# A two-layer metaformer on one core: another order of the pipeline's steps, other phases of the scan, one cast moved from GpSimd to VectorE

## The chip, the cores and the metric

One core of a Trainium2 chip runs the whole kernel. The metric is the device time of one execution in microseconds (us). The engines are called as in the profile: PE is TensorE's matmuls and PEld its weight loads, DVE is VectorE, ACT is ScalarE, POOL is GpSimd, SP is SyncE, which here only issues DMAs.

## The reference

The input x has shape (32, 56, 56, 96): 32 images of 56 by 56 positions with 96 channels. Two layers follow, each a mixing part and a feed-forward part with residual additions:

```python
# layer 0
x = x + L0_conv(ln_c(x))     # shifted 7x7 window attention, 3 heads of 32 channels
t = t + L0_ffn(ln_t(t))      # t: x as tokens
# layer 1
x = x + L1_conv(ln_c(x))     # layer norm, expansion to 192 channels, gate, scan along the width
t = t + L1_ffn(ln_t(t))
```

The attention rolls the image by three positions, makes q, k and v, adds a position bias to the scores, takes a softmax over the 49 positions of a window and projects the result. The feed-forward part rounds its operands to an 8-bit float, does 96 to 384 channels, relu, and 384 back to 96, with sums rounded to 16 bits:

```python
y = q_acc(einsum('bsk,nk->bsn', q_mul(x), q_mul(W)))
return q_acc(y + q_mul(b))
```

The scan of layer 1 is, for each image row and each of 192 channels, `state = state * A + u * B; y = sum(state * C)` over 56 columns. The result is multiplied by a sigmoid gate and projected back to 96 channels.

## The kernel before

**Tiles.** Each image is cut into four blocks of 14 rows, so there are 128 blocks of 784 positions. A block lies in one SBUF tile xb (128 partitions x 7 x 96, fp32), of which there are 14. It is loaded once, passes all steps of both layers in place, and is stored.

**Steps and shifts.** The work on one block is cut into about a hundred named steps. Each has a shift, written behind its name in the table PIPELINED: in tick t the step works on block t minus its shift. A tick goes through the table once, from front to back. The program is fully unrolled, and `in_order` fixes the order on each engine to that of the table. So a step early in the table with a shift of 2 runs beside steps of blocks that are 4, 6, 10 or 13 behind. The largest shift is 13, so the table is gone through 142 times; 13 ticks at each end fill and drain the pipeline.

**The names.** The letters a, f, e and g stand for the four layer norms: attention, first feed-forward, scan, second feed-forward. For each of them, s is the statistics (DVE, L535), m the subtraction of the mean (L541), n the multiplication with the root (L555), t the transposition into PSUM (PE, tr_a, tr_f, tr_e, tr_g: L217 or L566), and e or, for the scan, xe the copy out of PSUM (ACT; xe is L882 and writes xs). R0 to R7 compute the reciprocal roots of all four norms of a tick on DVE in eight small instructions (L509 to L517). The other steps are:

- Attention: q, k and v (PE, L616 and L635), eq, ek and ev (ACT copies, L628 and L646), sc (scores, L658, which takes two bank pairs), st0 to st2 (DVE, L687), ex0 to ex2 (ACT exponentials, L700), av (PE, L738), rc and an (DVE, L756 and L764), tro (PE, tr_o, L217), eo (ACT, L780), pr (PE, L793), ad (DVE adds pr to xb, L586).
- Feed-forward, with f or g behind the first letter: hf0 to hf2 (PE, ph_f, L815), xf (ACT cast to 16 bits, L827), rf (DVE bias and relu on the 16-bit tile h_f, L833), cf (cast to the 8-bit tile hq, L839), yf (PE, py_f, L849), zf (ACT, L861), bf and kf (additions, L867 and L871).
- Scan: pu0 to pu3 (PE, L896), th and uc (ACT out of pu into gt and u, L911 and L917), SC0 to SC5 (PE, the scan as matmuls with a Toeplitz matrix, L939), GA0 to GA5 (DVE, gate times scan, L959), gt0 and gt1 (PE transposition), eg1 and eg0 (ACT, L982), so (PE, L992), "as" (DVE adds so to xb, L586).
- LD loads a block and ST stores one, each with six or nine DMAs on SP's queue.

**Which engine.** ON_GPSIMD names the steps of the kinds m, n, c, b and k that POOL does. All others of these kinds are DVE's. Before, POOL does mf, nf, me, ne, ng, cf0, cf1, cf2 and kf.

**PSUM.** There are four pairs of PSUM banks (NPS = 4). When a PE step is put into the program, `banks` gives it the pair at the front of a free list. EMPTIES says after which step a pair is free again; then it goes to the end of that list. So the table also decides which emptying step a PE step has to wait for.

**The scan's phases.** A scan step SCn works on a window of four successive blocks at once, every fourth tick. PHASE gives, for each of the six groups of channels, at which block number modulo 4 the window begins. Phase 0 means that the window is one image. With any other phase it covers the end of one image and the beginning of the next, and the DVE step GA behind it needs four instructions instead of two. The tick of a scan step modulo 4 follows from its shift and its phase together.

**A second path.** The program contains another, unpipelined order (IN_TURN) behind a branch for weights of unusual size. It does not run on these inputs.

Of the kernel before, what the change touches and what calls it, by code (L numbers as in the profile page):

```python
# [52 lines left out]
ROOT_BITS = 1595932665.0  # L53
ROOT_STEPS = ((0.703952253, 1.681913974), (0.5, 1.50000032))

ON_GPSIMD = "mf nf me ne ng cf0 cf1 cf2 kf"


PIPELINED = (
    "xf0:4 xg0:13 bf:5 xg1:13 k:2 SC1:10 ne:6 ek:2 v:2 pr:3 GA1:10 ma:1 GA0:10 ad:3 q:2 te:6 hf2:4 sf:3 ev:2 "  # L60
    "eq:2 rf0:4 kf:5 mf:3 xe:6 sc:2 se:5 pu2:6 st0:2 xf2:4 st1:2 ex0:2 pu1:6 st2:2 ex1:2 R0:0 R1:0 rg1:13 "
    "ex2:2 th2:6 uc2:6 th1:6 rg0:13 uc1:6 gt1:10 gt0:10 R2:0 cg2:13 R3:0 cg0:13 av:2 eg1:10 hf1:4 rf2:4 "
    "tg:12 eg0:10 R4:0 pu0:6 cf0:4 cg1:13 R5:0 eg:12 mg:11 pu3:6 R6:0 R7:0 na:1 xf1:4 so:10 rc:2 an:2 nf:3 "
    "ta:1 rf1:4 cf2:4 uc0:6 th0:6 as:10 LD:0 sa:0 uc3:6 th3:6 tro:2 SC3:9 ea:1 SC2:9 SC4:9 ng:11 eo:2 SC5:9 "
    "tf:3 cf1:4 hg2:12 GA3:9 ef:3 xg2:12 sg:10 GA2:9 yg:13 GA5:9 GA4:9 yf:4 hf0:3 rg2:12 hg0:12 zg:13 bg:13 "
    "hg1:12 zf:4 me:5 kg:13 ST:13 SC0:9 "
)

IN_TURN = (
# [18 lines left out]
def kernel(  # L88
# [184 lines left out]
    ne = EH // 2  # L273
# [208 lines left out]
    def engine(name):  # L482
        return nc.gpsimd if name in ON_GPSIMD.split() else nc.vector

# [432 lines left out]
        nc.scalar.copy(dst, held["pu", i, j][:, 0:n, :, EH:].rearrange("p g r e -> p e g r"))  # L917


    PHASE = (3, 2, 1, 2, 3, 0)  # L920

    def window(n):
        return [i for i in range(n, n + NBLK) if 0 <= i < nblocks]
# [95 lines left out]
    def pipeline(text, track, one_bias):  # L1019
# [16 lines left out]
        for t in range(nblocks + 1 + max(lag for _, lag in table)):  # L1036
# [3 lines left out]
            for name, lag in table:  # L1040
                i = t - lag
                if name[0:2] in ("SC", "GA"):
                    due = (i - PHASE[int(name[2])]) % NBLK == 0 and window(i)
                elif name[0] == "R":
# [74 lines left out]
```

## Time and profile before

| | us |
|---|---|
| median of 3 runs | 3170.72 |
| lowest and highest run | 3163.45, 3171.2 |
| the profiled execution, its own time | 3165.43 |
| span of the profiled execution, first to last instruction | 3163.7 |
| PE busy in that span | 3042.9 |
| PEld, DVE, ACT, POOL busy | 2511.5, 2605.6, 2304.8, 1504.6 |

The granted TensorE clock was 0.989 of full speed in the mean.

A timeline row gives the start and the length of a group of like instructions in us, then engine, line, operation, out<-in with shapes, and the count; in brackets is the idle time of the engine before it and what ended it. A group's row gives its busy time in total and the mean length of one instruction in ns, then the idle time before it. A row of a stretch of time gives the stretch, its length, and the busy time of each engine.

### The profile page before, as it was taken

What the parts mean: (1) busy time and instruction counts of PE and PEld (TensorE: products, weight loads), DVE (VectorE), ACT (ScalarE), POOL (GpSimd) and SP (SyncE); (2) the same over time, 40 slices, a digit from 0 to 9 for tenths busy, and PEclk for the clock granted to TensorE, in tenths of its full rate; (3) what the DMA queues carried; (4) which work ended last, traced back from release to release, by engine and by line L of the source; (5) the groups of instructions that cost most, each with busy time, mean ns of one, the idle gap of its engine ahead of it and who ended that gap; (6) DMA issues with size and microseconds to landing.
All of it is one profiled execution on the core that took longest, in us unless ns stands there. A gap on an engine that the chain in (4) does not pass through costs nothing.

```text
span 3163.7 us, 180034 instructions
## 1 busy us (share of the span) xinstructions
PE 3042.9 (96%) x80228; PEld 2511.5 (79%) x80228; DVE 2605.6 (82%) x7149; ACT 2304.8 (73%) x4610; POOL 1504.6 (48%) x1219
## 2 busy tenths in 40 slices
PE   4999999999999999999999999999999999999996
PEld 3778888888888888888888888888888888888875
DVE  6778888888888888888888888888888888888876
ACT  2667777777777777777777777777777777777774
POOL 4555444445444445444444444544544544544540
PEclk8899999999999999999999999999999999999998
DMA  6000111111111111111111111111111111111001
GB/s 140 23 4 19 29 32 27 29 32 27 29 32 27 28 33 27 28 33 26 27 34 27 26 34 27 26 34 27 26 33 28 27 34 27 26 32 29 23 22 34
DMA packets 232640, 97.09 MB, mean 31 GB/s; under 512 B 225292, under 2 KB 231854, under 8 KB 231854
## 3 DMA queue, kind: packets, MB, share of 16 engines
q1 hardware_dynamic: 228410, 84.40, 11.5%
q8 instruction: 633, 10.37, 1.4%
q10 hardware_dynamic: 3444, 1.06, 0.2%
q14 instruction: 153, 1.25, 0.1%
HBM read 42.05 MB, written 43.35 MB: 27 GB/s over the span
## 4 chain that ended last, share of the span: by engine, by line
PE 90%; ACT 5%; DVE 2%; issue 2%; POOL 1%; DVEq 0%; ACTq 0%; DMA 0%; SPq 0%; POOLq 0%
PE pu L896 20%; PE so L992 10%; PE qk L616 9%; PE scan L939 7%; PE av L738 6%; PE pv L635 6%; PE s L658 5%; PE pr L793 5%; PE ph_g L815 4%; PE py_f L849 4%; PE py_g L849 4%; ACT qk L628 3%; PE gt L217 3%; PE ph_f L815 3%; PE tr_f L566 2%
## 5 line engine op out<-in xcount | busy, mean ns | idle before, releaser
L896 PE MATMUL pu<-weg,xs 128*64 128x192 f32 x7168 | 640.9, 330 | 4.1 <-ACT xs L882 3.5
L535 DVE BATCH_NORM_STATS2 stats<-xb 128x6 f32<-128x192 f32 x2048 | 578.1, 348 | 1.8 <-POOL xb L871 1.7
L555 POOL TENSOR_TENSOR xn_f<-xc_f,roots 128x672 fp8e5<-128x672 f32 x128 | 243.4, 1901 | 663.6 <-DVE roots L517 663.6
L896 PEld LDWEIGHTS pu<-weg,xs 128*64 128x64 f32 x7168 | 492.4, 137 | 81.4 <-ACT xs L882 6.0
L871 POOL TENSOR_TENSOR xb<-xb,y_f 128x672 f32<-128x672 f32 x128 | 239.3, 1870 | 464.6 <-DVE y_f L867 461.2
L541 POOL TENSOR_TENSOR xc_f<-xb,stats 128x672 f32<-128x672 f32 x128 | 181.6, 1419 | 426.9 <-DVE stats L535 270.2
L628 ACT COPY qk<-qk 128x392 f32<-128x392 f32 (+1 forms) x256 | 173.8, 679 | 231.9 <-PE qk L616 231.7
L992 PE MATMUL so<-wso,gT 128*64 128x96 f32 x7168 | 322.8, 248 | 4.8 <-ACT gT L982 4.8
L827 ACT CAST h_g<-ph_g 128x784 f16<-128x784 f32 x384 | 307.6, 856 | 27.3 <-PE ph_g L815 16.9
L827 ACT CAST h_f<-ph_f 128x784 f16<-128x784 f32 x384 | 318.4, 829 | 10.4 <-PE ph_f L815 10.4
L992 PEld LDWEIGHTS so<-wso,gT 128*64 128x64 f32 x7168 | 315.9, 138 | 10.2 <-ACT gT L982 5.4
L839 POOL CAST hq<-h_f 128x784 fp8e5<-128x784 f16 x384 | 320.3, 834 | 6.1 <-DVE h_f L833 6.1
L616 PE MATMUL qk<-xw,wqkv 128*32 128x196 f32 (+1 forms) x3072 | 304.8, 392 | 2.3 <-ACT h_f L827 2.3
L606 ACT COPY xw<-tr_a 96x392 f32<-96x392 f32 x256 | 117.4, 514 | 249.1 <-PE tr_a L217 212.6
L586 DVE TENSOR_TENSOR xb<-so,xb 128x384 f32<-128x384 f32 (+1 forms) x256 | 118.1, 503 | 188.8 <-PE so L992 188.8
L586 DVE TENSOR_TENSOR xb<-pr,xb 128x384 f32<-128x384 f32 (+1 forms) x256 | 118.1, 503 | 183.4 <-PE pr L793 183.4
L959 DVE SCALAR_TENSOR_TENSOR gt<-gt,scan 128x448 f32<-128x448 f32 (+2 forms) x694 | 236.5, 400 | 38.3 <-PE scan L939 38.1
L849 PEld LDWEIGHTS <-hq 128*128 128x128 fp8e5 x5376 | 246.7, 99 | 26.4 <-DVE hq L839 8.6
L939 PEld LDWEIGHTS scan<-u,toep 64*64 64x64 f32 x12288 | 200.1, 135 | 64.6 <-ACT xw L606 29.2
L939 PE MATMUL scan<-u,toep 64*64 64x56 f32 (+1 forms) x12288 | 221.6, 220 | 30.8 <-ACT xw L606 21.3
L917 ACT COPY u<-pu 128x384 f32<-128x384 f32 (+1 forms) x512 | 242.1, 473 | 4.5 <-PE pu L896 4.5
L911 ACT ACTIVATE gt<-pu 128x384 f32<-128x384 f32 (+1 forms) x512 | 237.8, 464 | 5.5 <-PE pu L896 5.5
(161 smaller groups left out, 6706.0 us busy)
## 6 DMA issues: line engine op xcount, KB each, us to landing
xb<-in_x_dram SPq DMA_DIRECT2D x224, 126.0 KB
out_dram<-xb SPq DMA_DIRECT2D x224, 126.0 KB
taps_d<-u SPq DMA_DIRECT2D x1, 4704.0 KB
xb<-in_x_dram SPq DMA_DIRECT2D x224, 13.1 KB
xb<-in_x_dram SPq DMA_DIRECT2D x224, 7.9 KB
out_dram<-xb SPq DMA_DIRECT2D x224, 13.1 KB
out_dram<-xb SPq DMA_DIRECT2D x224, 7.9 KB
xb<-in_x_dram SPq DMA_DIRECT2D x32, 72.0 KB
```

The source lines that it names most:

```text
L535: nc.vector.bn_stats(st[:, g : g + 2, :].rearrange("p g s -> p (g s)"), pair.rearrange("p g c -> p c g"))
L555: engine("n" + n).tensor_tensor(xn, xc, rs[:, :, None].to_broadcast([128, G, C]), ALU.mult, **saturate)
L616: nc.tensor.matmul(pq[j * rows : (j + 1) * rows, m, 0:size], wqkv[:, m * C + h0 * HD : m * C + h1 * HD], xws[i % 2][:, j * size : (j + 1) ...
L628: nc.scalar.copy(dst, held.pop(("qk", i, n)))
L827: nc.scalar.copy(h16.rearrange("p (h t) -> p h t", h=2), held.pop(("ph", n, i, hc))[:, :, 0:HALF])
L839: engine(f"c{n}{hc}").tensor_copy(hq[:, :, 0:HW], h16.rearrange("p (r w) -> p r w", w=HW), saturate=False)
L849: nc.tensor.matmul(po[:, g - g0, :], hq[hc][:, 2 * g : 2 * g + 2, :].rearrange("p r w -> p (r w)"), w2q[:, hc, :], start=(hc == 0), stop=( ...
L871: engine("k" + n).tensor_tensor(xtiles[i], xtiles[i], held.pop(("y16", n, i)), ALU.add)
L896: nc.tensor.matmul(pu[h * RS : (h + 1) * RS, g, r * E : (r + 1) * E], xs[:, 2 * j + g, r, :], weg[:, h, :], start=True, stop=True,)
L917: nc.scalar.copy(dst, held["pu", i, j][:, 0:n, :, EH:].rearrange("p g r e -> p e g r"))
L939: nc.tensor.matmul(py[o0 : o0 + RS, b, e, rows], toep[h * RS : (h + 1) * RS, ch * HW : ch * HW + RS], u[h * RS : (h + 1) * RS, ch, rows], ...
L992: nc.tensor.matmul(po[r * ROW : (r + 1) * ROW, g, :], gT[:, h, 2 * g + r, :], wso[:, h, :], start=(h == 0), stop=(h == 1),)
```

## The change

Three things differ; no instruction's form is new.

The table PIPELINED is another one, with the same step names. In it, all six scan groups have a shift of 9 (SC1, GA0 and GA1 had 10), v goes from 2 to 1, pr from 3 to 2, xf0 from 4 to 3, xg0 from 13 to 12, ne from 6 to 5, bf and kf from 5 to 4; most steps stand elsewhere in the order. PHASE has other values. ON_GPSIMD no longer names cf2, so that cast is DVE's.

```diff
-ON_GPSIMD = "mf nf me ne ng cf0 cf1 cf2 kf"
+ON_GPSIMD = "mf nf me ne ng cf0 cf1 kf"

 PIPELINED = (
-    "xf0:4 xg0:13 bf:5 xg1:13 k:2 SC1:10 ne:6 ek:2 v:2 pr:3 GA1:10 ma:1 GA0:10 ad:3 q:2 te:6 hf2:4 sf:3 ev:2 "
-    "eq:2 rf0:4 kf:5 mf:3 xe:6 sc:2 se:5 pu2:6 st0:2 xf2:4 st1:2 ex0:2 pu1:6 st2:2 ex1:2 R0:0 R1:0 rg1:13 "
-    "ex2:2 th2:6 uc2:6 th1:6 rg0:13 uc1:6 gt1:10 gt0:10 R2:0 cg2:13 R3:0 cg0:13 av:2 eg1:10 hf1:4 rf2:4 "
-    "tg:12 eg0:10 R4:0 pu0:6 cf0:4 cg1:13 R5:0 eg:12 mg:11 pu3:6 R6:0 R7:0 na:1 xf1:4 so:10 rc:2 an:2 nf:3 "
-    "ta:1 rf1:4 cf2:4 uc0:6 th0:6 as:10 LD:0 sa:0 uc3:6 th3:6 tro:2 SC3:9 ea:1 SC2:9 SC4:9 ng:11 eo:2 SC5:9 "
-    "tf:3 cf1:4 hg2:12 GA3:9 ef:3 xg2:12 sg:10 GA2:9 yg:13 GA5:9 GA4:9 yf:4 hf0:3 rg2:12 hg0:12 zg:13 bg:13 "
-    "hg1:12 zf:4 me:5 kg:13 ST:13 SC0:9 "
+    "ev:2 ma:1 q:2 ad:3 k:2 sf:3 xg1:13 te:6 hf2:4 rf0:4 se:5 eq:2 ek:2 sc:2 xe:6 R0:0 st2:2 xf2:4 ex2:2 "
+    "st0:2 pu2:6 st1:2 ex0:2 th2:6 pu0:6 uc2:6 rg0:13 R1:0 gt1:10 rg1:13 th0:6 mf:3 R2:0 ex1:2 me:5 cg2:13 "
+    "R3:0 cg1:13 R4:0 rf2:4 cg0:13 eg1:10 gt0:10 R5:0 eg0:10 uc0:6 pu1:6 th1:6 uc1:6 R6:0 av:2 LD:0 hf1:4 "
+    "tg:12 R7:0 so:10 eg:12 xf1:4 na:1 rc:2 an:2 mg:11 pu3:6 as:10 rf1:4 uc3:6 cf0:4 th3:6 cf2:4 hg2:12 ta:1 "
+    "sg:10 tro:2 SC3:9 xg2:12 SC4:9 ea:1 eo:2 GA3:9 SC5:9 SC0:9 GA0:9 GA4:9 nf:3 tf:3 GA5:9 yg:13 cf1:4 "
+    "hg0:12 yf:4 ne:5 ef:3 zg:13 rg2:12 xg0:12 zf:4 hg1:12 hf0:3 ng:11 sa:0 bg:13 SC2:9 kg:13 xf0:3 bf:4 "
+    "SC1:9 ST:13 v:1 kf:4 GA2:9 pr:2 GA1:9 "
 )
 
-    PHASE = (3, 2, 1, 2, 3, 0)
+    PHASE = (0, 0, 1, 2, 1, 3)
```

## The prediction

> **What bounds the kernel now.** First part 1 of the page, then two steady ticks out of the stretches' busy times, from one tr_e step to the next (columns after the length: PE, PEld, DVE, ACT, POOL busy with counts, granted clock, DMA).
>
> ```profile
> PE 3042.9 (96%) x80228; PEld 2511.5 (79%) x80228; DVE 2605.6 (82%) x7149; ACT 2304.8 (73%) x4610; POOL 1504.6 (48%) x1219
> 1514.34:1537.50 23.16, 22.86 (x595) 18.89 (x594) 19.39 (x54) 17.80 (x36) 11.69 (x9) 1.00 0.13 31
> 1537.50:1561.78 24.28, 23.97 (x659) 19.92 (x658) 20.67 (x58) 17.98 (x36) 11.14 (x9) 1.00 0.14 34
> ```
>
> PE is all but full at full clock; the second tick holds one scan more (1.09 us). Four such ticks (one period of the scans) take 23.16 + 24.28 + 24.24 + 23.18 = 94.86 us, 128 blocks 32 x 94.86 = 3036 us; the other 128 us of the 3163.7 us span are the filling and the draining.
>
> A busy PE hides short waits, because a matmul's modelled end runs on. So in the timeline I measure each step from its first matmul to that of the next step.
>
> ```profile
> 1514.34 0.55 PE L217 MATMUL tr_e<-ident,xc_e 56*96 56x56 f32 x14
> 1514.51 0.82 ACT L628 COPY qk<-qk 128x784 f32<-128x784 f32 x1 [1.72 <-PE qk L616]
> 1514.83 0.51 PE L815 MATMUL ph_f<-xq,w1q 128*128 128x392 fp8e5 x2
> 1515.22 1.24 ACT L882 ACTIVATE xs<-tr_e,bet,gam 96x392 f32<-96x392 f32 x2
> 1515.38 1.24 PE L658 MATMUL s<-qk 32*64 32x49 f32 x96
> ...
> 1521.66 0.51 PE L815 MATMUL ph_f<-xq,w1q 128*128 128x392 fp8e5 x2
> 1522.01 0.50 PE L566 MATMUL tr_g<-ident,xn_g 128*96 128x112 fp8e5 x7
> ...
> 1526.97 0.92 DVE L586 TENSOR_TENSOR xb<-so,xb 128x384 f32<-128x384 f32 x2 [1.33 <-PE so L992]
> 1527.24 0.54 PE L217 MATMUL tr_o<-ident,an 49*96 49x49 f32 x16
> 1528.04 1.15 PE L939 MATMUL scan<-u,toep 64*64 64x56 f32 x64 [0.26 <-DVE xb L586]
> ...
> 1531.96 0.83 PE L815 MATMUL ph_g<-xq,w1q 128*128 128x392 fp8e5 x4
> 1532.75 0.87 PE L616 MATMUL qk<-xw,wqkv 128*32 128x196 f32 x16
> ```
>
> Three waits return in every tick. Step hf2 takes 0.55 us before sc (1514.83 to 1515.38), hf1 only 0.35 (1521.66 to 1522.01): 0.21 us lost, because q stands two short steps ahead of sc and eq (0.82) is not done. tro takes 0.80 us where its shortest of 128 is 0.47: 0.33 lost, because the scan takes the banks that "as" empties (1526.97 + 0.92). hg0 and hg1 take 0.79 us where two such steps take 0.67: 0.12 lost at hg1, which waits for zg. Together 0.66 us a tick. All other steps have the same length, within about 0.01 us, in nearly all ticks: PE sets the pace and these waits are all that a new order can win in the steady part.
>
> **A rule of the Trainium skill beside this.** "Perfetto Trace Analysis", Identifying the Most-Contended Engine, says that matmul busy overstates how full TensorE is, and takes the weight loads' busy share instead: 18.89 of 23.16 us. By that, up to 4.27 us a tick (547 us) would be open. The rows decide otherwise: steps do not get shorter when neighbours change, so the sum uses 0.66 us.
>
> **The change, part by part.** The words speak of three exchanges; the list ON_GPSIMD loses one name, cf2. All else is order.
>
> Scans. Six windows per four ticks before and after, but in ticks of 3, 1, 1, 1 before and 2, 2, 1, 1 after; two of them now cover one image instead of one. An unsplit window's two instructions of 606 ns cost DVE 1.21 us, a split one's 2 x (494 + 261) = 1.51: 32 x 0.30 = 10 us less DVE. One window at the edge of the batch falls away, 1.1 us of PE.
>
> cf2. POOL loses 128 x 834 ns = 107 us, DVE gains 128 x 561 ns = 72 us (the same form's row hq<-h_g):
>
> ```profile
> L839 POOL CAST hq<-h_f 128x784 fp8e5<-128x784 f16 x384 | 320.3, 834 | 6.1 <-DVE h_f L833 6.1
> L839 DVE CAST hq<-h_g 128x784 fp8e5<-128x784 f16 x384 | 215.4, 561 | 0.0
> 1524.59 0.83 POOL L839 CAST hq<-h_f 128x784 fp8e5<-128x784 f16 x1
> 1524.59 1.05 DVE L833 TENSOR_SCALAR h_f<-h_f,b1q 128x784 f16<-128x784 f16 x1
> ```
>
> The last two lines show rf1 needing 1.05 us instead of 0.42 (the 1520.39 row's length) while POOL casts cf2: it ends 0.22 us after POOL does. In the new order rf1 meets an idle POOL (cf1 waits for rf1): 0.63 us less DVE a tick.
>
> A rule that speaks against the change: "SBUF — State Buffer", Who interferes with whom, has VectorE and GpSimd share a port pair as an exclusive lock; the later of the two stands still for the other's whole instruction, and casts, tensor_scalar and two-input operations on VectorE are concerned. The row above agrees. By the rule I look at each such DVE step against POOL's new order (mf me cf0 nf cf1 ne ng kf): cf2 starts before cf1, so POOL waits; rg2 arrives in ng, about 0.6 us; R0 in mf's end, 0.2; ma in kf in two ticks of four, 0.4. Together 1.0 us a tick. DVE then needs 20.0 (mean of four ticks) + 0.56 - 0.63 - 0.08 + 1.0 = 20.9 of 23 us. Without the lock it would be 19.9; neither reaches PE's pace, so these lie beside PE as long as DVE's waits come in the right places.
>
> Order. Origin is q's first matmul; PE steps keep their lengths above, without the three waits: q 0, k 1.42, te 2.22, hf2 2.70, sc 3.03, pu2 4.18, pu0 5.56, gt1 6.93, gt0 7.28, pu1 7.75, av 9.09, hf1 10.62, tg 10.96, so 11.39, pu3 13.80, hg2 14.47, ta 14.80, tro 15.19, scan 15.66, tf 16.75, yg 17.13, hg0 18.02, yf 18.35, hg1 19.25, hf0 19.58, second scan (two ticks of four) 19.92, v, pr, end 22.44 or 23.53. Handovers by the rows: PE to ACT 0.17 to 0.25, PE to DVE 0.12, back to PE 0.05 to 0.1; neighbours on ACT or DVE overlap by about 0.1. A bank pair goes to the step that asks next after its emptying step, so the table tells who waits for whom. The places with least room:
> - sc and pu2: eq 1.59, then ek, then xe to 4.1; sc needs 2.9 (has 3.03), pu2 needs about 4.1 (4.18). k now stands between q and sc, 0.80 us on PE against ek's 0.48 on ACT. Wait one goes, 0.1 to spare.
> - tro takes the banks of "as": so ends 13.80, "as" 13.92 to 14.84, needed 15.19. Before, 0.86 us of PE steps lay between so and the taker, now pu3, hg2 and ta, 1.39. Wait two goes, 0.2 to 0.3 to spare, if DVE is there; its order (an, mg, as) has it free at 12.8.
> - hg1 takes ef's banks (18.3, needed 19.25), hf0 those of zg (19.0, needed 19.58). Wait three goes.
> - v or the second scan takes xg0's: hg0 ends 18.35, ACT is at xg0 from 18.9 to 19.7, needed 19.92.
> - yf takes those of the scan's additions GA: 16.75 + 0.12 + 1.3 = 18.2, needed 18.35. DVE does as, rf1, cf2, sg first, free at 16.7. If cf2 came a POOL cast (0.83) late, PE would lose 0.65 there.
> - te takes ad's: pr ends 0, DVE does bf, in two ticks a GA, ma, then ad to 1.4 at most, needed 2.22.
> - gt1 takes those of st1: sc ends 4.18, three rows 1.7 us, 6.0, needed 6.93.
> kf stays on POOL, one tick earlier behind bf; se (2.3) needs it, and it ends at 1.5 or before. On SP, ST (6 or 9 DMAs) still follows kg, LD (as many) waits behind it for the store of the same buffer: store issue to load issue was 3.2 us (1510.33 to 1513.57), so sa at 19 has some 10 us.
>
> Sum: waits removed 128 x 0.66 = 84 us; new short ones where the room is 0.1, taken at 0.1 us a tick (bounds 0 and 0.4): +13; filling and draining: v and pr a tick earlier into PE's idle time (1.37 + 1.16) and the lost window, -3. The profiled execution took 3165.4 us: 3165 - 84 + 13 - 3 = 3091. The median shown is 5 us above that execution: **3096 us**.
>
> **Rivals.**
> Half the gain: the three places with 0.1 to 0.2 us of room (xe to pu2, xg0 to v, GA to yf) miss by as much again, 0.35 us a tick, 45 us: 3126. For it: handovers vary by 0.1. Against: they hardly vary between ticks.
>
> Slower: the port lock. If POOL runs later against DVE than laid out, cf2, rg2, ma and R0 each stand behind nearly whole instructions (0.83, 1.42, 1.47, 1.42: 5.1 us a tick) and not 1.0 to 1.4. DVE's idle time before GA (0.3) and st2 (0.65) and gt1's room (0.8) absorb 1.8 us more; beyond that PE stops at gt1. It decides from 1.8 + 0.66 = 2.5 us more; at 2.9, PE loses 1.1 us a tick, 141 us: 3170 - 84 + 141 = 3227. For it: rf1's row. Against: POOL is idle half of each tick and starts each piece on DVE's word.
>
> No change: new waits by chance equal the old, 3165 to 3175.
>
> **How the numbers follow.** Forecast 0.62, half the gain 0.18, no change 0.04, slower 0.16. A measurement tells about 0.3% (10 us). Faster 0.80, same 0.04, slower 0.16. The forecast's own range is 3074 (no new wait) to 3112 (0.25 us a tick); reaching over the half gain to no change, 3072 to 3172 leaves out 0.16 above and some 0.04 below.
>
> **What would show it.** Right: ticks of 22.5 and 23.6 us, hf2 0.34, tro below 0.5, no scan step waiting for xb; rf1 near 0.42 us; DVE idle still before "as". Wrong: pu steps waiting for ACT xs, yf's banks for DVE gt, or R0 and rg2 rows of a microsecond with gt1 late behind st1. Other PE step lengths under new neighbours would also break the sum.

## The result, and the profile after

The changed kernel takes 3137.45 us (median of 6 runs, 3130.2 to 3145.13), the kernel before 3170.96 us beside it (3163.45 to 3179.87). The ratio is 0.9891, 95% interval 0.9869 to 0.9912: 33.5 us faster, where 75 were forecast. The time lies outside the forecast's own range (3074 to 3112), inside its wide one (3072 to 3172), and nearest to its rival of half the gain (3126), but the reason is not that rival's, whose number came near by luck.

The page of the changed kernel, and the busy time by tick (length; then PE, PEld, DVE, ACT, POOL busy; clock; DMA share; GB/s). A tick begins here at q's first matmul:

```profile
PE 3053.4 (97%) x80164; PEld 2472.0 (79%) x80164; DVE 2681.6 (86%) x7213; ACT 2339.4 (75%) x4610; POOL 1408.4 (45%) x1091
```

```profile
1524.85:1547.81 22.96, 22.96 (x598) 18.57 (x595) 20.15 (x55) 18.25 (x37) 9.69 (x8) 1.00 0.11 25
...
1570.77:1594.76 23.99, 23.99 (x662) 19.55 (x658) 20.85 (x55) 18.26 (x37) 11.85 (x9) 1.00 0.15 35
...
sum 93.96, PE 93.96 PEld 76.30 DVE 82.11 ACT 72.84 POOL 43.09; mean PE 23.49 PEld 19.08 DVE 20.53 ACT 18.21 POOL 10.77
```

PE has no idle time left in a tick: 93.96 of 93.96 us, where it had some 0.3 us a tick before. And yet the ticks are 22.96 and about 24.0 us, not the 22.5 and 23.6 that the forecast's sum gave. So nothing of the missing time shows as idle. That alone does not rule out waits, since a busy PE can hide a short one; the step lengths have to tell. Four ticks went from 94.86 to 93.96 us, 32 x 0.90 = 29 us, which is the gain of the profiled execution (span 3163.7 to 3135.6, 28 us).

The timeline of PE in one tick (start, busy, out<-in, tile and shapes). A step's length is the distance to the next row's start:

```profile
1527.55 0.51 PE L815 MATMUL ph_f<-xq,w1q 128*128 128x392 fp8e5 x2
1527.98 1.27 PE L658 MATMUL s<-qk 32*64 32x49 f32 x96
1529.18 2.82 PE L896 MATMUL pu<-weg,xs 128*64 128x192 f32 x32
1531.93 0.89 PE L217 MATMUL gt<-ident,gt 56*96 56x56 f32 x28
1532.76 1.52 PE L896 MATMUL pu<-weg,xs 128*64 128x192 f32 x16
1534.21 1.60 PE L738 MATMUL av<-v,pT 64*64 64x33 f32 x96
...
1536.52 2.53 PE L992 MATMUL so<-wso,gT 128*64 128x96 f32 x56
1538.88 0.82 PE L896 MATMUL pu<-weg,xs 128*64 128x192 f32 x8
1539.64 0.51 PE L815 MATMUL ph_g<-xq,w1q 128*128 128x392 fp8e5 x2
1540.08 0.55 PE L217 MATMUL tr_a<-ident,xc_a 56*96 56x56 f32 x14
1540.46 0.55 PE L217 MATMUL tr_o<-ident,an 49*96 49x49 f32 x16
1540.94 1.16 PE L939 MATMUL scan<-u,toep 64*64 64x56 f32 x64
```

The last steps of the same tick, where hf0 (ph_f) now stands ahead of v (pv):

```profile
1544.52 0.50 PE L815 MATMUL ph_g<-xq,w1q 128*128 128x392 fp8e5 x2
1544.86 0.49 PE L815 MATMUL ph_f<-xq,w1q 128*128 128x392 fp8e5 x2
1545.28 1.54 PE L635 MATMUL pv<-wqkv,xw 128*64 128x96 f32 x32
```

And in the kernel before, hg2 ahead of yg, hf0 ahead of hg0, and pu2 with pu1 ahead of gt:

```profile
1506.35 0.50 PE L815 MATMUL ph_g<-xq,w1q 128*128 128x392 fp8e5 x2
1506.69 1.05 PE L849 MATMUL py_g<-w2q,hq 128*128 128x96 fp8e5 x21
...
1508.47 0.50 PE L815 MATMUL ph_f<-xq,w1q 128*128 128x392 fp8e5 x2
1508.81 0.83 PE L815 MATMUL ph_g<-xq,w1q 128*128 128x392 fp8e5 x4
...
1516.55 2.82 PE L896 MATMUL pu<-weg,xs 128*64 128x192 f32 x32
1519.31 0.89 PE L217 MATMUL gt<-ident,gt 56*96 56x56 f32 x28
```

The reader is to look at the number pair before the shapes: 128\*128, 32\*64, 128\*64 are rows by columns of the array that a matmul uses, its tile. tro (tr_o) is down to 0.48 us, as forecast, and the scan follows with no wait. hf2 (ph_f before s) takes 0.43, not 0.34. hg2 (ph_g), which now stands between pu3 and ta, takes 0.44 where it took 0.34 among its like; so does hf0, 0.42 for 0.34. pu1 alone takes 1.45, where pu2 and pu1 together took 2.75.

All differences of PE's steps, medians over the whole trace (from each step's first matmul to that of the next), before and after:

| step | before | after | difference |
|---|---|---|---|
| hf2 | 0.557 | 0.438 | -0.12 |
| tro | 0.800 | 0.476 | -0.32 |
| hg0 + hg1 | 0.792 | 0.672 | -0.12 |
| hg2 | 0.336 | 0.438 | +0.10 |
| hf0 | 0.336 | 0.424 | +0.09 |
| the four pu and so | 7.163 | 7.316 | +0.15 |
| sum in a tick | | | -0.22 |

128 x 0.22 = 28 us, the gain of the profiled execution again; every other step kept its median length within 0.01 us. The agreement is rougher than it looks: the ticks at both ends are not steady, and medians leave out rare pauses of PE (below), which between 300 and 2900 us make 6 us in the kernel before and 1 us in the changed one. With them the mean of 96 steady ticks went from 23.77 to 23.51 us. The first three rows are what the forecast counted (it took 0.21, 0.33 and 0.12), the last three what it held fixed.

### The profile page after: what moved, and what is told of

Same layout as the page of the kernel before. It is cut to its first block, busy times and chain, and to the rows that moved or that the text cites. A ratio compares the mean times of both kernels' runs of the same rounds, so it can differ in the third digit from the quotient of the medians.

```text
span 3135.6 us, 180306 instructions
## 1 busy us (share of the span) xinstructions
PE 3053.4 (97%) x80164; PEld 2472.0 (79%) x80164; DVE 2681.6 (86%) x7213; ACT 2339.4 (75%) x4610; POOL 1408.4 (45%) x1091
## 4 chain that ended last, share of the span: by engine, by line
PE 96%; DVE 2%; POOL 1%; ACT 1%; issue 0%; SPq 0%; DMA 0%; ACTq 0%; POOLq 0%; DVEq 0%
PE pu L896 20%; PE so L992 10%; PE qk L616 9%; PE scan L939 6%; PE av L738 6%; PE pv L635 6%; PE ph_f L815 5%; PE s L658 5%; PE pr L793 5%; PE ph_g L815 4%; PE py_f L849 4%; PE py_g L849 4%; PE gt L217 3%; PE tr_a L217 2%; PE tr_f L566 2%; PE tr_e L217 2%
## 5 line engine op out<-in xcount | busy, mean ns | idle before, releaser
L896 PE MATMUL pu<-weg,xs 128*64 128x192 f32 x7168 | 663.3, 330 | 4.6 <-ACT xs L882 3.7
L839 POOL CAST hq<-h_f 128x784 fp8e5<-128x784 f16 x256 | 248.7, 972 | 497.6 <-DVE h_f L833 497.6
L871 POOL TENSOR_TENSOR xb<-xb,y_f 128x672 f32<-128x672 f32 x128 | 224.5, 1754 | 378.9 <-DVE y_f L867 375.6
L992 PEld LDWEIGHTS so<-wso,gT 128*64 128x64 f32 x7168 | 302.6, 138 | 13.8 <-ACT gT L982 5.2
L687 DVE SCALAR_TENSOR_TENSOR pT<-s,bias 128x196 f32<-128x196 f32 (+1 forms) x512 | 213.5, 459 | 88.2 <-PE s L658 74.3
L628 ACT COPY qk<-qk 128x784 f32<-128x784 f32 (+1 forms) x256 | 166.1, 650 | 148.3 <-PE qk L616 146.5
L959 DVE SCALAR_TENSOR_TENSOR gt<-gt,scan 128x448 f32<-128x448 f32 (+1 forms) x632 | 234.7, 428 | 35.4 <-PE scan L939 32.4
L700 ACT ACTIVATE pT<-pT 128x392 f32<-128x392 f32 x384 | 194.8, 528 | 74.2 <-DVE pT L687 74.0
L616 PEld LDWEIGHTS qk<-xw,wqkv 128*32 128x32 f32 (+1 forms) x3072 | 120.6, 119 | 136.9 <-issue 127.6
L738 PEld LDWEIGHTS av<-v,pT 64*64 64x64 f32 x12288 | 193.4, 136 | 44.1 <-issue 33.3
```

The costliest lines, as they stand in the source:

```text
L616: nc.tensor.matmul(pq[j * rows : (j + 1) * rows, m, 0:size], wqkv[:, m * C + h0 * HD : m * C + h1 * HD], xws[i % 2][:, j * size : (j + 1) ...
L738: nc.tensor.matmul(po[r * 64 : r * 64 + 64, k, n0 : n0 + HD + 1], pT[kp, h, pair * W2 : pair * W2 + 64], v[kp, pair * NH + h, :], start=Tr ...
L839: engine(f"c{n}{hc}").tensor_copy(hq[:, :, 0:HW], h16.rearrange("p (r w) -> p r w", w=HW), saturate=False)
L896: nc.tensor.matmul(pu[h * RS : (h + 1) * RS, g, r * E : (r + 1) * E], xs[:, 2 * j + g, r, :], weg[:, h, :], start=True, stop=True,)
L959: nc.vector.scalar_tensor_tensor(part, part, 1.0, py[:, b, :, rows].rearrange("p e q -> p q e"), op0=ALU.add, op1=ALU.mult,)
L992: nc.tensor.matmul(po[r * ROW : (r + 1) * ROW, g, :], gT[:, h, 2 * g + r, :], wso[:, h, :], start=(h == 0), stop=(h == 1),)
```

## The experiments

Three theories. **A:** PE loses some 0.1 us or more whenever a step follows one of another tile; part of what I had called waits was this, and the new order has two more such changes in a tick (15 for 13: pu1 stands between gt and av, hg2 between pu3 and ta; in this count 128\*96 goes with 128\*128, as hf1 takes 0.346 us ahead of tg and 0.336 is its like's length, and 56\*96 with 49\*96). **B:** the longer steps are waits for bank pairs or data that a busy PE hides. **C:** VectorE and GpSimd standing behind each other ate the gain.

### The two true waits, one by one and together

x9, k behind q; x5, pu3 behind so; x59, both; each in the kernel before. The edits of x9 and x5, cut out of the table:

```diff
-k:2 SC1:10 ne:6 ek:2 v:2 pr:3 GA1:10 ma:1 GA0:10 ad:3 q:2 te:6 hf2:4 sf:3 ev:2 eq:2 rf0:4
+SC1:10 ne:6 v:2 pr:3 GA1:10 ma:1 GA0:10 q:2 ad:3 k:2 sf:3 ev:2 te:6 hf2:4 eq:2 ek:2 rf0:4
```

```diff
-mg:11 pu3:6 R6:0 R7:0 na:1 xf1:4 so:10 rc:2
+mg:11 R6:0 R7:0 na:1 xf1:4 so:10 pu3:6 rc:2
```

> The kernel before with k moved behind q alone (v, pr, q, k, te, hf2, sc; ek follows eq), so that eq has k's 0.80 us more before sc asks for it. The number of places where neighbouring PE steps differ in their tile of rows by columns stays the same. Theory A (a change of tile costs PE some 0.09 to 0.12 us, and that is a part of what I took for a wait): hf2 goes from 0.557 to 0.44 us, 128 x 0.12 = 15 us less, about 3156. The forecast's own reading (all of hf2's 0.21 us was a wait): hf2 goes to 0.35, 27 us less, about 3144. If the order of k and q does nothing: 3171.

> The kernel before with pu3 moved behind so alone: between so and tro there are now pu3 and ta (1.13 us) where there was ta (0.38), so 'as' has emptied so's banks when the step after tro asks for them. The tiles of the neighbours do not change (pu, so, pu are all 128 rows by 64 columns; then ta as before). The forecast's reading and theory A agree: tro goes from 0.80 to 0.48 us, 128 x 0.32 = 41 us less, about 3130. If the wait only moves to another step, as in a rival where DVE is late with 'as': 3160 to 3171.

> Both single moves in the kernel before: k behind q and pu3 behind so. Theory A: the two true waits of 0.12 and 0.32 us go and nothing else changes, 128 x 0.44 = 56 us less, about 3115, which is below the changed kernel (3137) with none of its other moves. The forecast's reading: 128 x (0.21 + 0.33) = 69 us less, about 3102. If the two gains share one cause, less than their sum: 3130.

Measured: x9 3158.5 us, ratio 0.9975 (0.9965 to 0.9985); x5 3131.5, 0.9884 (0.9864 to 0.9905); x59 3135.3, 0.9899 (0.9881 to 0.9918), beside 3167.9 of the kernel before.

In x9 hf2 goes from 0.557 to 0.437 us, not to 0.35: of the 0.21 that the forecast called a wait, 0.12 was one, and 0.09 stays with k's 0.80 us between. PE in x9:

```profile
1511.49 0.51 PE L815 MATMUL ph_f<-xq,w1q 128*128 128x392 fp8e5 x2
1511.92 1.24 PE L658 MATMUL s<-qk 32*64 32x49 f32 x96
```

The time fell by 9 and not by 15; PE now paused in more ticks than before (below). In x5 the wait at tro goes whole. The timeline of PE in x5:

```profile
1537.52 2.48 PE L992 MATMUL so<-wso,gT 128*64 128x96 f32 x56
1539.83 0.82 PE L896 MATMUL pu<-weg,xs 128*64 128x192 f32 x8
1540.58 0.55 PE L217 MATMUL tr_a<-ident,xc_a 56*96 56x56 f32 x14
1540.96 0.54 PE L217 MATMUL tr_o<-ident,an 49*96 49x49 f32 x16
1541.43 1.16 PE L939 MATMUL scan<-u,toep 64*64 64x56 f32 x64
```

tro takes 0.47 us, and that is worth 36 us, more than the changed kernel's 33.5: one moved step, with no new change of tile, does what the whole new order does. x59 missed: hf2 and tro are both short, but 24 of the 56 us did not come.

### One more change of tile, alone; and one fewer

xs, the kernel before with pu1 between gt and av; x1b, the changed kernel with pu1 behind so; x1c, the same with ex1 earlier on ACT.

```diff
-pu2:6 st0:2 xf2:4 st1:2 ex0:2 pu1:6 st2:2 ex1:2 R0:0 R1:0 rg1:13 ex2:2 th2:6 uc2:6 th1:6 rg0:13 uc1:6 gt1:10 gt0:10
+pu2:6 st0:2 xf2:4 st1:2 ex0:2 st2:2 ex1:2 R0:0 R1:0 rg1:13 ex2:2 th2:6 uc2:6 rg0:13 gt1:10 gt0:10 pu1:6
```

The edit of x1b, and that of x1c on top of it:

```diff
-R2:0 ex1:2 me:5 cg2:13 R3:0 cg1:13 R4:0 rf2:4 cg0:13 eg1:10 gt0:10 R5:0 eg0:10 uc0:6 pu1:6 th1:6 uc1:6 R6:0 av:2 LD:0 hf1:4
-tg:12 R7:0 so:10 eg:12 xf1:4 na:1 rc:2 an:2 mg:11 pu3:6
+R2:0 ex1:2 me:5 cg2:13 R3:0 cg1:13 R4:0 rf2:4 cg0:13 gt0:10 av:2 eg1:10 R5:0 eg0:10 uc0:6 R6:0 LD:0 hf1:4
+tg:12 R7:0 so:10 eg:12 xf1:4 pu1:6 na:1 rc:2 an:2 mg:11 pu3:6 th1:6 uc1:6
```

```diff
-st1:2 ex0:2 th2:6 pu0:6 uc2:6 rg0:13 R1:0 gt1:10 rg1:13 th0:6 mf:3 R2:0 ex1:2 me:5
+st1:2 ex0:2 ex1:2 th2:6 pu0:6 uc2:6 rg0:13 R1:0 gt1:10 rg1:13 th0:6 mf:3 R2:0 me:5
```

> The kernel before with one step of the changed order: pu1 stands between gt and av, no longer behind pu2 (th1 and uc1 move behind av with it). One more change of tile in each tick (pu to gt to pu to av, where it was pu to gt to av). Theory A: the pu steps take 1.42 + 1.45 us where they took 2.75, 128 x 0.117 = 15 us more, about 3186. If the longer step pu1 in the changed kernel was a wait for its banks or for the emptying of av's (rival B): nothing here, where DVE's and ACT's order around it is that of before, 3171, or a wait shown as idle PE.

> The changed kernel with pu1 taken from between gt and av and put behind so, ahead of pu3 (av, gt0, th1 and uc1 moved with it): pu1 then stands between two steps of its own tile, and gt is followed by av as in the kernel before. Theory A: the pu steps after so take 2.1 us where they took 1.45 + 0.75, 128 x 0.10 = 13 us less, about 3124. Rival B (pu1's 1.45 us were a wait for banks or for ACT): it stays at 1.45 or another step takes the wait over, 3137 or more.

> The run with pu1 behind so, with the third part of the exponent (ex1) put ahead of th2 on ScalarE. Without that, av waited for it in every tick, 1.676 against 1.535 us, since pu1 no longer stood between. Theory A: av goes back to 1.535, 128 x 0.14 = 18 us less than 3157, about 3139; the pu steps keep their 2.05 us (2.20 in the changed kernel), and what keeps it from 3137 - 19 = 3118 are pauses within av, since gt and av are neighbours again, some 20 us. If no pauses: about 3120. If av's 0.14 us was a change of tile and no wait: 3157.

Measured: xs 3182.8 us, 1.0051 (1.0034 to 1.0069): 15 us slower, as theory A said; theory B said nothing or idle PE. PE in xs:

```profile
1525.12 1.52 PE L896 MATMUL pu<-weg,xs 128*64 128x192 f32 x16
1526.57 0.89 PE L217 MATMUL gt<-ident,gt 56*96 56x56 f32 x28
1527.40 1.52 PE L896 MATMUL pu<-weg,xs 128*64 128x192 f32 x16
1528.85 1.60 PE L738 MATMUL av<-v,pT 64*64 64x33 f32 x96
```

1.45 + 1.45 us for what took 2.75 in one piece: 0.15 us for one more change, with no idle time in front of either.

x1b took 3157.3 us (0.9960, 0.9943 to 0.9976), 20 slower than the changed kernel where 13 less were expected. The pu steps behind did what A said (pu1 and pu3 together 2.05 where they took 1.45 + 0.75 = 2.20), but av went from 1.535 to 1.676 us: without pu1 ahead of it, it waited for the last exponent on ACT (128 x 0.14 = 18 us), and PE pauses besides, as below (some 15 us). The wait came with my edit, and x1c takes it away: av is 1.535 again in most ticks, the pu steps stay at 2.05, and the time is 3136.8 us (0.9905, 0.9888 to 0.9922). pu1 and pu3 in x1c:

```profile
1535.52 2.12 PE L896 MATMUL pu<-weg,xs 128*64 128x192 f32 x24
1537.58 0.51 PE L815 MATMUL ph_g<-xq,w1q 128*128 128x392 fp8e5 x2
```

The 19 us of the joined pu steps are still not to be seen in the time, because this kernel pauses as x59 does: between 300 and 2900 us, 20 av steps are longer by 16 us in sum, some other steps by 6.

### The cost of a change by itself

m1 runs PE alone, in one execution: pairs of two kinds of matmul, in blocks of 4 and of 32. It leaves out the whole reference and copies the input to the output. Its loop, where a kind is rows, columns, data type and moving columns (96 throughout), and r0 and c0 alternate between the halves of the array that the tile leaves room for:

```python
while done < EACH:
    for k, (rows, cols, d, size) in enumerate(kinds):
        for m in range(block):
            ...
            nc.tensor.matmul(
                pq[k][c0 : c0 + cols, m % 2, 0:size],
                w[r0 : r0 + rows, 0:cols],
                w[r0 : r0 + rows, 128 : 128 + size],
                start=True, stop=True,
            )
    done += block
```

> No part of the reference is computed: PE alone, with the input copied to the output. Nine pairs of two kinds of matmul (96 columns moving), 128 of each kind, once in blocks of 4 that alternate and once in blocks of 32, so 56 more changes of kind in the first (63 against 7). No matmul waits for another engine. Theory A: a pair whose tiles of rows by columns differ costs about 56 x 0.09 to 0.12 = 5 to 7 us more in blocks of 4 than in blocks of 32; the pairs of one tile (128*64 with itself, and 128*128 in f32 and in fp8) cost nothing more. If the data type is what matters, the pair of f32 and fp8 with one tile costs as much as the others. Rival B (the longer steps were waits for banks or other engines): no pair costs more.

PE's timeline of one pair, 128\*64 and 64\*64, in short blocks and in long ones (each f32 matmul is two rows):

```profile
152.26 0.56 PE L60 MATMUL p_a<-w 128*64 128x96 f32 x8
152.75 0.40 PE L60 MATMUL p_b<-w 64*64 64x96 f32 x8
153.07 0.56 PE L60 MATMUL p_a<-w 128*64 128x96 f32 x8
...
176.79 2.78 PE L60 MATMUL p_a<-w 128*64 128x96 f32 x62
179.50 1.55 PE L60 MATMUL p_b<-w 64*64 64x96 f32 x64
180.98 2.91 PE L60 MATMUL p_a<-w 128*64 128x96 f32 x64
```

Short blocks take 0.49 and 0.32 us, 0.81 a pair. An eighth of the long ones (2.84 and 1.48, the medians) is 0.54 a pair. The difference of 0.27 us is 1.75 changes (two against a quarter), 156 ns each, the two directions of a pair taken together. By the same sum from the medians of each pair:

| pair | ns for one change |
|---|---|
| 128\*64 with itself (other tile name, other bank) | 0 (both 0.330 us for 4) |
| 128\*128 f32 with 128\*128 fp8 | 20 |
| 128\*64 f32 with 128\*128 fp8 | 128 |
| 128\*64 with 128\*32 | 140 |
| 128\*64 with 32\*64, 64\*64 | 155, 156 |
| 128\*64 with 128\*128, 64\*128 | 160, 161 |
| 64\*64 with 64\*128 | 166 |

No other engine works there once w is filled, so it is no wait for banks: that a change of tile costs is shown, and for pu1 B is out (xs, x1c). That the extra 0.10 us of hg2 and 0.09 of hf0 are such changes is concluded from their size and from their keeping it within 0.003 us in every steady tick; neither step was moved alone. In the one tile tried with both data types, 128\*128, the type hardly matters. The records of weight loads show where the time goes: among like tiles the next weight load starts some 0.16 us ahead of its matmul, under the matmuls that still run; across a change it starts with its own first matmul, 0.25 us after the start of the old tile's last matmul (changed kernel: last pu matmul 1533.952, av's first weight load 1534.206, its first matmul 1534.207). The Trainium skill has the rule, without a price: "TensorEngine Tiling (Array Packing)", Key Properties, says that a change of tiling mode drains TensorE. The price here is 0.13 to 0.17 us bare, and 0.09 to 0.15 in the kernel; that it is a drain is the page's word, while the late weight load is what the trace shows.

### The cast, and the shifts

x6, the changed kernel with cf2 on GpSimd; x7, the changed kernel with the old shifts; x59p, x59 with the new shifts (the second diff below, the other way round).

```diff
-ON_GPSIMD = "mf nf me ne ng cf0 cf1 kf"
+ON_GPSIMD = "mf nf me ne ng cf0 cf1 cf2 kf"
```

```diff
-    PHASE = (0, 0, 1, 2, 1, 3)
+    PHASE = (3, 2, 1, 2, 3, 0)
```

> The changed kernel with the cast cf2 back on GpSimd, the table and the shifts as changed. Theory A: PE has no wait on DVE to lose, so the cast's place is worth nothing, 3132 to 3142, unless cf1, which then stands 0.83 us of GpSimd later, comes late for yf: up to 0.65 us a tick more, 83 us. Rival C (the cast and VectorE's standing behind GpSimd ate the missing gain): 20 to 40 us less, about 3100 to 3117.

> The changed kernel with the old shifts of the scan (three windows in one tick of four), all else as changed. If DVE sets the end of the tick of three windows (two additions of 1.2 to 1.5 us more than in a tick of one, and cf2 is DVE's here as well): 0.8 to 1.3 us more in one tick of four, 32 times, 26 to 42 us more, 3160 to 3175. The forecast put the shifts at nothing but the edge of the batch: 3137 to 3139.

> The kernel before with the two moves (k behind q, pu3 behind so) and, as its only other edit, the changed kernel's shifts of the scan: two windows in two ticks of four and one in the others, where it was three and one. In the two moves without it PE waited 0.84 us behind av in the tick of three windows, 32 x 0.84 = 27 us. Theory A with DVE as the cause of that wait: it goes, 3168 - 128 x 0.44 = about 3111, below both kernels. If the wait behind av is not due to the three windows: 3135 as without it.

x6: 3131.4 us, 0.9877 (0.9855 to 0.9899), which its interval does not tell from the changed kernel. The cast's place is worth nothing that can be measured, and C, which gave it 20 to 40 us, is out. What C is about does happen, but beside PE. DVE and POOL of the changed kernel:

```profile
1539.10 0.92 DVE L586 TENSOR_TENSOR xb<-so,xb 128x384 f32<-128x384 f32 x2 [1.16 <-PE so L992]
1539.94 0.41 DVE L833 TENSOR_SCALAR h_f<-h_f,b1q 128x784 f16<-128x784 f16 x1
1540.27 0.56 DVE L839 CAST hq<-h_f 128x784 fp8e5<-128x784 f16 x1
1540.42 1.11 POOL L839 CAST hq<-h_f 128x784 fp8e5<-128x784 f16 x1 [3.97 <-DVE h_f L833]
1542.76 1.31 POOL L555 TENSOR_TENSOR xn_g<-xc_g,roots 128x672 fp8e5<-128x672 f32 x1
1543.36 0.93 DVE L833 TENSOR_SCALAR h_g<-h_g,b1q 128x784 f16<-128x784 f16 x1
```

rf1 takes 0.41 us, POOL's cf1 1.11 because cf2 on DVE is ahead of it, rg2 0.93 because it meets ng on POOL, all as forecast. DVE still stands idle 1.16 us ahead of "as".

x7: 3183.2 us, 1.0041 (1.0027 to 1.0054), 46 us slower than the changed kernel. x59p: 3176.2 us, 1.0016 (1.0005 to 1.0026), 41 slower than x59 where 24 less were expected. Both miss for one reason. PE in a tick of x7, then of x59p:

```profile
625.43 2.09 PE L939 MATMUL scan<-u,toep 64*64 64x56 f32 x128
...
630.14 1.05 PE L849 MATMUL py_f<-w2q,hq 128*128 128x96 fp8e5 x21 [0.68 <-DVE gt L959]
```

```profile
1531.45 2.09 PE L939 MATMUL scan<-u,toep 64*64 64x56 f32 x128
...
1535.02 1.05 PE L849 MATMUL py_g<-w2q,hq 128*128 128x96 fp8e5 x21 [0.68 <-ACT xq L807]
```

x128 is two windows in one place. A table with the other's shifts lets two scans follow each other directly, and py then waits for the additions or for ACT. In x59p the steps hg and py are together 0.3 us a tick longer than in x59, in x7 0.4 longer than in the changed kernel, which is the loss. So the new shifts lose with the old table's scans, and the new table loses with the old shifts; they fit only together. The wait behind av in x59, for which x59p was made, was no matter of three windows either.

### Where x59's gain went: pauses that wait for nothing

PE's timeline in x59:

```profile
1502.38 0.89 PE L217 MATMUL gt<-ident,gt 56*96 56x56 f32 x28
1503.20 1.59 PE L738 MATMUL av<-v,pT 64*64 64x33 f32 x93
1505.35 0.30 PE L738 MATMUL av<-v,pT 64*64 64x33 f32 x3 [0.55 <-issue]
1505.58 0.51 PE L815 MATMUL ph_f<-xq,w1q 128*128 128x392 fp8e5 x2
```

PE stops within one step, three matmuls before its end: no semaphore, no data. 28 av steps between 300 and 2900 us are longer by 0.3 to 1.2 us, 18 us in sum, and some pu steps by 5 more. The kernel before has 6 us of such pauses in the same stretch, so they explain some 18 of the 24 us. The trace has the transfers of the instruction queue (634 of 16 KB, one for each 250 or so of PE's recorded instructions). Each long pause begins about 200 PE instructions after the start of such a transfer and ends 1.2 to 1.6 us after its end (here: 1503.02 to 1503.94, PE goes on at 1505.35). This fits a PE that stands without instructions; no run shows it directly. Transfers that start 0.4 to 0.8 us ahead of av are the ones at risk: 19 of 20 came with a pause in x59, 15 of 16 in x1c, 11 of 14 in x9, 5 of 8 in the kernel before, 3 of 9 in x5, and none of 12 in the changed kernel. (This stretch was chosen after the fact; in x59s, below, 8 of 8 such transfers came with a pause, but they account for only 8 of its 26.) Two attempts at the cause:

> The kernel before with k behind q, pu3 behind so, and pu1 between gt and av (three moves of the changed kernel's order, with the old shifts and cf2 on GpSimd). In the two moves alone PE paused in some 30 ticks within av or pu, 0.5 to 1.2 us each, some 24 us in all, waiting for no engine; each pause came about 200 PE instructions after the start of a transfer on the instruction queue and ended 1.2 to 1.5 us after that transfer. gt and av are PE's densest stretch (248 instructions in 2.36 us). If instruction supply is the cause, pu1 between them (32 matmuls and weight loads in 1.45 us more) removes the pauses in av, and one more change of tile costs 15 us: 3168 - 56 + 15 = about 3127. If the pauses have another cause and stay: about 3150.

> The run with k behind q and pu3 behind so, without the transfers of the steady part: only the first 14 blocks are loaded and only the last 14 stored; the blocks between work on what the buffers hold, so their results are not computed from x. It is a test of the pauses alone. In the run of matmuls alone PE paused 0.7 to 3.1 us six times while the copy kept the DMA engines full (the first 60 us) and not once in 400 us without it. If the blocks' loads and stores hold up the instruction transfers: no pauses within av and pu from about 350 to 2800 us, 3168 - 128 x 0.44 = about 3112, of which some 3 us of pauses at the two ends remain. If the pauses come from where the instruction pages' limits fall alone: they stay in some 25 ticks, about 3135.

x59s, with xs's edit on top of x59, took 3152.2 us (0.9956, 0.9940 to 0.9972), the number for pauses that stay: 22 long ones within av although pu1 stands between gt and av. That gt and av stand close together is not the cause. x59d,

```diff
+        if i < NX:
             for dst, src in block_dmas(i, x, xb):
...
+        if i >= nblocks - NX:
             for src, dst in block_dmas(i, out, xb):
```

took 3135.6 us (0.9887, 0.9863 to 0.9912): with the DMA engines 2% busy in four ticks where x59 has 10 to 13%, the pauses stand in nearly the same ticks as in x59 (at 375, 446, 586, 658 us in both). The blocks' transfers are not the cause either. In m1 PE paused six times, 11.4 us in sum and 2.9 at most, while its copy filled the DMA engines, and not once after; x59d says that this does not carry over. Where in a tick these transfers fall was not varied by itself. Why pauses follow in one order and not in another at the same place stays open.

## Why the prediction was wrong, point by point

- **What bounds the kernel**: right. PE sets the pace before and after; each run's time moved with PE's steps.
- **"Three waits return in every tick", 0.66 us**: right in mechanism, wrong in size. tro's 0.33 was a wait and went (x5: 36 us). Of hf2's 0.21, 0.12 was one (x9); the rest has the size of a change of tile, which hf2 has ahead of sc. Of hg1's 0.12, 0.09 was none: it was the change of tile ahead of k, and with k gone from there it came back at hf0, +0.09, where v follows. The other 0.03 went; whether it was the wait for zg stays open (in x9, where v or a scan follows hg1 in place of k, all 0.12 stay).
- **"PE steps keep their lengths above"**: this is the step that failed. I had compared steps in one order only, where each had always the same neighbours, and took their constancy between ticks for a property of the step. The new order puts pu1 between gt and av, +0.15 (measured alone in xs: +0.15), hg2 between pu3 and ta, +0.10, and hf0 ahead of v, +0.09 us a tick.
- **The new short waits, +0.10**: none came: the places named as having least room held, and no step grew that does not stand at a change of tile.
- The sum: forecast -0.66 + 0.10 = -0.56 us a tick. Of the difference to -0.22, hf2 makes 0.09, tro 0.01, hg1 and hf0 together 0.09 (forecast -0.12, came -0.03), pu1 and hg2 0.25; the waits that did not come give 0.10 back. Together 0.34 us, and 128 x 0.34 = 44 us; 41.5 are missing by the medians, 46 by the profiled executions (3091 forecast, 3137.61 taken). The range did not follow from the sum either: with no new wait it gives 3096 - 13 = 3083, not 3074.
- **"Perfetto Trace Analysis" of the Trainium skill, set aside (it names a second measure, MFU, too) because "steps do not get shorter when neighbours change"**: that sentence was wrong. Steps do, by 0.10 to 0.15 us for a change of tile less. The 4.27 us a tick were still no forecast: the gap stayed in the changed kernel, where weight loads are busy for 76.30 of 93.96 us and PE has no idle time. The page that bears on the case is the one on tiling, which I did not weigh.
- **The cast, the lock on DVE, the shifts**: the lengths came as worked out (rf1 0.41 for 0.42; rg2 0.93; DVE 20.5 us a tick for 20.9), and beside PE, so worth nothing. "-3" for the shifts holds only because the table was made for them (x7: +46).
- **The rivals**: half the gain came nearest, 11 us off, with the wrong cause (short rooms that miss). The slower one didn't begin: DVE's wait ahead of "as" shows its room.
- The text did name "other PE step lengths under new neighbours" as what would break the sum; it gave that no price and no chance, though the trace of before held it: of hg0 and hg1, the same work, hg0 took 0.34 us ahead of a like step and hg1 0.46 ahead of k, of which 0.09 was the change.

## What to carry to other kernels

When an order of TensorE steps is changed, list the tile (rows by columns) of each step in both orders and count the changes; in these runs each cost 0.09 to 0.17 us, showed as busy and not as idle, and a reordering that removes a wait by separating like tiles gives part of it back. Before a step's excess is called a wait, look at a step of the same kind that has nothing to wait for and the same change of tile behind it: what it has too much as well is no wait. One step moved for the largest wait alone (x5) was worth as much as the whole new table, so price the parts of a reordering singly.

## What the runs showed of the hardware that was not expected

- A change of tile cost PE 0.13 to 0.17 us bare, and a change of data type (f32 and fp8) in the tile 128\*128 0.02 (m1).
- PE can pause in straight-line code with nothing in the profile to wait for: 0.3 to 1.2 us each, some 37 times in x59 between 300 and 2900 us, 24 us in sum. The long pauses stand at a fixed distance from transfers of the instruction queue (they end 1.2 to 1.6 us after one). The Trainium skill, "Runtime: NRT & Kernel Launch", Instruction fetch mechanics, calls the cost of crossing a 16 KiB boundary of the instruction stream "mostly hidden". If these pauses are that cost, the changed kernel agrees (1 us) and x59, x1c, x59s and x59d do not (22 to 29 us). Whether they come depends on small moves of the order, by more than most of these moves are worth.
